# A two-layer graph network on one core: pairwise distances from a broadcast through DRAM, and seven block products for all four gate columns

## Chip, core and metric

The kernel runs on one core of a Trainium2 chip. The metric is the device time of one execution in microseconds (us). Five engines work side by side: TensorE (PE; its weight loads are listed apart as PEld), VectorE (DVE), ScalarE (ACT), GpSimd (POOL) and SyncE (SP). SP, ACT and POOL also start DMAs, and a DMA's waits stand in the queue of the engine that starts it. All data is 32-bit float.

## What is computed

There are 64 graphs of 256 nodes with 256 features. Layer 0 is a degree-normalised convolution with a residual and a layer norm. Layer 1 takes its output `x` and the mask `adj`:

```python
h = relu(bn(conv1d(xc, conv1_w)))                 # xc = x transposed, width 1
x_conv = relu(bn(conv1d(h, conv2_w)) + xc)        # width 17 along the nodes
s = x @ w_se.T + b_se                             # 3 columns
dist = |s_n - s_m|^2                              # 256 x 256 per graph
A = exp(-dist) * adj
x_nmp = A @ relu(x @ w_msg.T + b_msg)
gi = [x_conv, x_nmp] @ w_ih.T + b_ih              # 3 x 256 columns: r, z, n
gh = x @ w_hh.T + b_hh
r, z = sigmoid(gi_r + gh_r), sigmoid(gi_z + gh_z)
n = tanh(gi_n + r * gh_n)
out = layernorm(x + (1 - z) * n + z * x)
```

The gates thus need four column groups of 256: r and z (both inputs summed), n from `gi` and n from `gh`.

## The kernel before

**Stages.** The width-17 convolution is done by Fourier transforms over all graphs of a quarter (`Q` = 16 graphs) at a time, four quarters in all. For each quarter, graphs first pass `layer0` (L346) and `layer1` (L431), which leaves the transformed `h` in a large tile, and the inputs of the gates in DRAM (`xn_d`, `x1_d`). Then `products` (L557) multiplies the frequencies by weights streamed from DRAM (`load_u`, L529), in twelve steps; `real_transform`, `complex_begin` and `complex_end` (L731) transform back on VectorE alone and write `xc_d`; last, `gru` (L832) computes the gates of each graph and stores the output.

**Overlap.** These stages are Python generators that yield after each piece, and the end of the file interleaves their pieces. While one quarter is multiplied and transformed back, the first `AHEAD` graphs of the next one run, into a second tile `V2` (12 graphs ahead in the first quarter, 6 in the next two); the other graphs of that quarter follow with four "early" gates; the other twelve gates ("late") go beside the next quarter's products and transform. `paced` (L942) places pieces of the transform after marked instructions: each `mark` adds 1.2, 1.0, 0.65 or 1.35 pieces (`RATES`, L1042). What is then left of the transform is run without such cover (L1087 to L1090). The fourth quarter's sixteen gates run alone at the end.

**The order on each engine** is not just the order of the code. A planner lays out each engine's queue ahead of the run, from the order of the code and from estimated durations; in the trace VectorE runs L906 of a gate ahead of its L888, which the code has first. On the chip each queue is then worked off in order: an instruction that waits holds everything behind it.

**Distances** (L449 to L506). `scols` takes the three columns of `s` and their negative half-norms; PE transposes it (L493), ACT and VectorE copy the two halves to SBUF (L495, L497), two matmuls of 32 rows give the products (L504), ACT takes exp (L505), VectorE multiplies by the transposed `adj` in `adjT` (L506), and PE forms `x_nmp` in the same graph (L513). `xn_d` is written in one DMA from ACT's queue (L518).

**Gates** (L832 to L911). The columns r and z are one 2 x 2 block product by Strassen's method: seven block products of three matmuls of 256 columns each (L846), with four input sums on POOL (L825 to L830) and four weight differences. The two n groups are plain: twelve matmuls of 256 columns (L883). All accumulate in a PSUM pool of four banks (`accbank`), and VectorE adds the parts. `trz`, `nn`, `first` and `gn` hold the gate values; the layer norm of the output (L313) ends the chain.

The compiler splits every such matmul in two instructions in the trace, so 33 matmuls of a gate are 66 instructions.

Of the kernel before, what the change touches and what calls it, by code (L numbers as in the profile page):

```python
# [9 lines left out]
F32 = mybir.dt.float32  # L10
AF = mybir.ActivationFunctionType
ALU = mybir.AluOpType
# [14 lines left out]
def kernel(  # L27
# [93 lines left out]
    vectors = const.tile([16, P], F32, name="bn_in")  # L121
# [21 lines left out]
    scols = const.tile([P, NCH, P], F32, name="scols")  # L143
    nc.gpsimd.memset(scols, 0.0)
    for c in (NSE, 32 + NSE):
        nc.gpsimd.memset(scols[:, :, c : c + 1], 1.0)
# [4 lines left out]
    wrz = const.tile([P, 7, HALF, D], F32)  # L151
    B11, B21, B22, T1, T2, T3, T4 = range(7)
    wn = const.tile([P, 3 * DCH, D], F32)
    brz_t = const.tile([P, 2, D], F32)
    bn_t = const.tile([P, 2, D], F32)
# [53 lines left out]
    def tables(pool):  # L209

        period = pool.tile([1, 25 * FL], F32, name="period")
# [8 lines left out]
        fwd_row = pool.tile([1, FL, FL], F32, name="fwd_row")  # L220
        w_row = pool.tile([1, TAPS, 2, NU], F32, name="w_row")
# [30 lines left out]
        row = w_row.rearrange("p t h n -> p t (h n)")  # L252
        for c in range(GC):
            nc.sync.dma_start(wt[c * TR : (c + 1) * TR], row[:, :TR])
        nc.sync.dma_start(wt[GC * TR :], row[:, TR : TR + 1].to_broadcast([1, GC, 2 * NU]))
# [85 lines left out]
    XN = {}  # L341
    ALONE = set()
# [3 lines left out]
    def layer0(g):  # L346
# [3 lines left out]
        adjT = work.tile([P, NCH, 3, P], F32, name="adjT", bufs=3)  # L350
# [71 lines left out]
    def x1_transposed(g):  # L422
        x1 = X1.pop(g)
        xn = XN[g] = work.tile([P, 2 * DCH, N], F32, name="xn")
        p = bank("p_x1T").rearrange("p (k n) -> p k n", k=DCH)
        for k in range(DCH):
            for c in range(NCH):
                nc.tensor.transpose(p[:, k, c * P : (c + 1) * P], x1[:, c, k * P : (k + 1) * P], ident)
        nc.scalar.copy(xn[:, :DCH], p)  # L429

    def layer1(g, place):  # L431

        if g not in XN:
            x1_transposed(g)
        xn, adjT = XN.pop(g), ADJT.pop(g)
        x1T = xn[:, :DCH]
        yield

        h = work.tile([P, NCH, D + NSE], F32, name="h", bufs=1)
        for c in range(NCH):  # L440
# [5 lines left out]
            mark(nc.vector.tensor_tensor(h[:, c, :], p, bc1, op=ALU.add))  # L446
        nc.scalar.activation(h[:, :, :D], h[:, :, :D], AF.Relu)  # L447

        s3 = h[:, :, D:]  # L449
        cols = scols.rearrange("p c (q r) -> p c q r", r=32)  # L450
        nc.vector.tensor_copy(cols[:, :, :, :NSE], s3.unsqueeze(2).to_broadcast([P, NCH, 4, NSE]))
        sq3 = small.tile([P, NCH, NSE], F32, name="sq3")
        nc.vector.scalar_tensor_tensor(sq3, s3, -1.0, s3, op0=ALU.mult, op1=ALU.mult)
        nsq = small.tile([P, NCH], F32, name="nsq")
        nc.vector.tensor_reduce(nsq, sq3, AX.X, ALU.add)
        nc.vector.tensor_scalar(
            cols[:, :, 2:4, NSE], nsq.unsqueeze(2).to_broadcast([P, NCH, 2]), 0.5, None, op0=ALU.mult
        )
        yield
        msg = work.tile([P, NCH, D], F32, name="msg", bufs=1)  # L460
# [7 lines left out]
        nc.scalar.activation(msg, msg, AF.Relu)  # L468
        yield
# [19 lines left out]

        yield  # L490
        p = bank("p_rows")
        for c in range(NCH):
            nc.tensor.transpose(p[:, c * P : (c + 1) * P], scols[:, c, :], ident)  # L493
        dl = work.tile([64, N], F32, name="dist_l", bufs=1)
        nc.scalar.copy(dl, p[0:64, :N])  # L495
        dr = work.tile([64, N], F32, name="dist_r", bufs=1)
        nc.vector.tensor_copy(dr, p[64:P, :N])  # L497
        yield

        aT = work.tile([P, NCH, 2, P], F32, name="aT", bufs=1)  # L500
        for c in range(NCH):
            rows = slice(32 * c, 32 * c + 32)
            p = bank("p_dist")[:, :N]
            nc.tensor.matmul(p, dl[rows, c * P : (c + 1) * P], dr[rows, :], start=True, stop=True)  # L504
            nc.scalar.activation(aT[:, c].rearrange("p n q -> p (n q)"), p, AF.Exp, bias=nsq[:, c : c + 1], scale=2.0)  # L505
        mark(nc.vector.tensor_mul(aT, aT, adjT[:, :, 0:3:2, :]))  # L506
        yield
        if g in ALONE:
            x1_transposed(g + 1)
        p = bank("p_nmp").rearrange("p (k n) -> p k n", k=DCH)  # L510
        for k in range(DCH):
            for mc in range(NCH):
                nc.tensor.matmul(  # L513
                    p[:, k, :], msg[:, mc, k * P : (k + 1) * P], aT[:, mc].rearrange("p n q -> p (n q)"),
                    start=mc == 0, stop=mc == NCH - 1,
                )
        nc.scalar.copy(xn[:, DCH:], p)
        nc.scalar.dma_start(xn_d[g], xn)  # L518
# [114 lines left out]
    def turned(re, im, angle):  # L633


        t = freq.tile([P, 2, D], F32, name="turn", bufs=3)
# [7 lines left out]
    def real_transform():  # L644
# [17 lines left out]
        for i, x, y in ((1, 9, 13), (2, 10, 14), (3, 15, 11)):  # L662
            angle = math.pi * ORDER[i] / 8
            t = freq.tile([P, 2, D], F32, name="turn", bufs=3)
# [50 lines left out]
    def output(q, n, re, im):  # L715
# [4 lines left out]
        t = freq.tile([P, 2, D], F32, name="turn", bufs=3)  # L720
# [79 lines left out]
    def transposed(g):  # L800
# [3 lines left out]
        if in_blocks(g):  # L804
            behind(nc.vector.transpose(xcT.rearrange("p k (s r) -> p k s r", r=RB), CONV.pop(g)))
            nc.gpsimd.tensor_tensor(xcT, xcT, inputs[:, :DCH], op=ALU.add)
# [15 lines left out]
    def input_sums(g):  # L822
# [9 lines left out]
    def gru(g):  # L832
# [41 lines left out]
        for c in range(NCH):  # L874
            terms = [(inputs[:, k, c * P : (c + 1) * P], wn[:, k]) for k in range(3 * DCH)]
            if c == 0 and following:
                input_sums(g + 1)
# [280 lines left out]
```

## Time and profile before

| | |
|---|---|
| median of 3 runs | 2149.64 us (2147.59 to 2150.93) |
| span of the profiled execution, first to last instruction | 2152.3 us |
| PE, PEld busy | 2052.7 us, 1735.8 us |
| DVE, ACT, POOL busy | 1581.6, 841.9, 664.8 us |
| moved by DMA | 298.30 MB, 139 GB/s on average |
| granted TensorE clock | 0.990 on average |

The profile lists no separate time for the profiled execution other than its span, which lies 2.7 us (0.12%) above the median of the runs; sums below are made against the span. Busy time is the union of an engine's instructions. A matmul of 128x256 is listed with some 380 ns, but consecutive ones overlap, so what one takes of PE is the distance between starts. "Releaser" means the work whose end released a wait.

### The profile page before, as it was taken

How to read it: one execution, taken by the hardware profiler on the slowest of the kernel's cores; microseconds unless marked ns; L12 is line 12 of the kernel's file. 1: busy time of each engine (PE TensorE's matmuls, PEld its weight loads, DVE VectorE, ACT ScalarE, POOL GpSimd, SP SyncE). 2: the span in 40 equal slices, each digit the busy share in tenths (PEclk: the TensorE clock that was granted, in tenths of full speed). 3: DMA queues.
4: the chain of work that ended last, by engine and by line, in shares of the span. 5: the costliest groups of instructions: out<-in, count | busy, mean ns of one | idle time of the engine just before them, and what ended most of it. 6: DMA issues, size and time to landing. Idle time of an engine off the chain costs nothing.

```text
span 2152.3 us, 28977 instructions
## 1 busy us (share of the span) xinstructions
PE 2052.7 (95%) x9693; PEld 1735.8 (81%) x9693; DVE 1581.6 (73%) x3719; ACT 841.9 (39%) x1857; POOL 664.8 (31%) x640
## 2 busy tenths in 40 slices
PE   7999999887999999899999999999999998999997
PEld 5888788776888888788888888777888887788886
DVE  5555578775568788775656988876566889988887
ACT  4665643456431123445552122446553112222222
POOL 2444310121431244213322133323231123444442
PEclk9999999999999999999999999999999999999999
DMA  4766666434346644233326654324324744443331
GB/s 122 235 196 197 198 194 207 142 132 134 96 146 203 203 110 128 93 112 113 113 94 190 205 157 113 118 98 133 102 88 136 243 116 122 119 102 99 94 84 54
DMA packets 295085, 298.30 MB, mean 139 GB/s; under 512 B 76414, under 2 KB 273618, under 8 KB 294938
## 3 DMA queue, kind: packets, MB, share of 16 engines
q1 hardware_dynamic: 235050, 200.46, 30.9%
q10 hardware_dynamic: 44480, 67.39, 8.8%
q0 software_dynamic: 15408, 28.61, 6.1%
q8 instruction: 77, 1.26, 0.2%
q14 instruction: 70, 0.57, 0.1%
HBM read 193.28 MB, written 103.06 MB: 138 GB/s over the span
## 4 chain that ended last, share of the span: by engine, by line
PE 44%; DVE 12%; issue 9%; POOL 6%; ACT 4%; DMA 2%; ACTq 0%; SPq 0%; POOLq 0%; DVEq 0%
PE p_rz L846 14%; PE p_n L883 8%; PE p_k L539 7%; PE p_out L409 2%; PE p_nmp L513 2%; PE p_hT L399 2%; PE p_dft L480 2%; POOL ln_rs L323 2%; PE p_conv L443 1%; PE p_msg L464 1%; PE p_dist L504 1%; POOL sums L826 1%; POOL sums L825 1%; DMA u<-ud 1%; POOL xc_g L796 1%
## 5 line engine op out<-in xcount | busy, mean ns | idle before, releaser
L883 PE MATMUL p_n<-wn,inputs 128*128 128x256 f32 x1536 | 355.1, 385 | 13.4 <-DVE first L859 13.2
L846 PE MATMUL p_rz<-wrz,sums 128*128 128x256 f32 x1536 | 348.6, 380 | 1.3 <-DVE gn L888 0.8
L883 PEld LDWEIGHTS p_n<-wn,inputs 128*128 128x128 f32 x1536 | 288.5, 192 | 64.2 <-DVE first L859 20.9
L846 PEld LDWEIGHTS p_rz<-wrz,sums 128*128 128x128 f32 x1536 | 290.0, 190 | 44.5 <-issue 5.2
L846 PE MATMUL p_rz<-wrz,inputs 128*128 128x256 f32 x1152 | 271.6, 379 | 1.0 <-ACT inputs L808 1.0
L323 POOL TENSOR_TENSOR ln_rs<-ln_rs,neg_half 128x2 f32<-128x2 f32 x129 | 99.1, 768 | 510.9 <-DVE ln_rs L322 464.0
L846 PEld LDWEIGHTS p_rz<-wrz,inputs 128*128 128x128 f32 x1152 | 217.6, 190 | 31.1 <-ACT inputs L808 1.2
L895 ACT ACTIVATE nn<-gn 128x256 f32<-128x256 f32 x128 | 53.3, 417 | 332.1 <-DVE gn L892 331.7
L539 PE MATMUL p_k<-u,VM 128*128 128x256 f32 x736 | 175.2, 380 | 2.7 <-DMA u<-ud 1.9
L369 POOL TENSOR_TENSOR dis<-deg,neg_half 128x2 f32<-128x2 f32 x64 | 46.1, 720 | 423.6 <-DVE deg L367 393.1
L333 ACT ACTIVATE x_g<-x_g,ln_mr,ln_rs 128x256 f32<-128x256 f32 x128 | 70.0, 593 | 241.5 <-DVE ln_mr L331 241.5
L539 PEld LDWEIGHTS p_k<-u,VM 128*128 128x128 f32 x736 | 138.1, 190 | 24.4 <-DMA u<-ud 4.1
L480 PE MATMUL p_dft<-fwd,h 128*128 128x240 f32 x512 | 120.2, 379 | 25.9 <-ACT h L447 24.6
L399 PE MATMUL p_hT<-adjT,x 128*128 128x256 f32 x512 | 129.8, 397 | 14.0 <-DVE adjT L381 7.6
L825 POOL TENSOR_TENSOR sums<-inputs 128x384 f32<-128x384 f32 x64 | 67.1, 1048 | 239.0 <-ACT inputs L816 206.3
L480 PEld LDWEIGHTS p_dft<-fwd,h 128*128 128x128 f32 x512 | 95.2, 192 | 47.6 <-ACT h L447 41.2
L506 DVE TENSOR_TENSOR aT<-aT,adjT 128x512 f32<-128x512 f32 x64 | 44.6, 698 | 118.2 <-ACT aT L505 118.1
L443 PE MATMUL p_conv<-wc,xn 128*128 128x259 f32 x512 | 125.8, 388 | 4.3 <-ACT xn L429 4.3
L392 POOL TENSOR_TENSOR x_t<-x_t,b_t 128x512 f32<-128x512 f32 x64 | 85.4, 1334 | 142.6 <-ACT x L391 97.4
L409 PE MATMUL p_out<-w,hT 128*128 128x256 f32 x512 | 123.1, 383 | 1.4 <-ACT hT L404 0.7
L464 PE MATMUL p_msg<-wmsg,xn 128*128 128x256 f32 x512 | 121.4, 380 | 0.0
L513 PE MATMUL p_nmp<-aT,msg 128*128 128x256 f32 x512 | 121.2, 379 | 0.2 <-DVE aT L506 0.2
(157 smaller groups left out, 3910.2 us busy)
## 6 DMA issues: line engine op xcount, KB each, us to landing
u<-ud SPq DMA_DIRECT2D x284, 256.0 KB
xn_d<-xn ACTq DMA_DIRECT2D x64, 512.0 KB
inputs<-xn_d SPq DMA_DIRECT2D x64, 512.0 KB
ud<-u_set POOLq DMA_DIRECT2D x39, 480.0 KB, 6.1
adj_t<-in_adj_dram SPq DMA_DIRECT2D x64, 256.0 KB
x_t<-in_x_dram SPq DMA_DIRECT2D x64, 256.0 KB
x_d<-x ACTq DMA_DIRECT2D x64, 256.0 KB
xc_d<-VM SPq DMA_DIRECT2D x64, 256.0 KB
```

The source lines that it names most:

```text
L323: nc.gpsimd.tensor_tensor(rs[:, : len(chunks)], rs[:, : len(chunks)], neg_half[:, : len(chunks)], op=ALU.pow)
L392: nc.gpsimd.tensor_tensor(x_t, x_t, b0_t.unsqueeze(1).to_broadcast([P, NCH, D]), op=ALU.add)
L399: nc.tensor.matmul(p[:, k, :], x1[:, mc, k * P : (k + 1) * P], adjT[:, mc, 1 - mc : 3 - mc, :].rearrange("p n q -> p (n q)"), start=mc == ...
L409: nc.tensor.matmul(p[:, c, :], hT[:, k, c * P : (c + 1) * P], w0[:, k, :], start=k == 0, stop=k == DCH - 1)
L443: nc.tensor.matmul(p, x1T[:, k, c * P : (c + 1) * P], wc1[:, k, :], start=k == 0, stop=k == DCH - 1)
L464: nc.tensor.matmul(p[:, c, :], x1T[:, k, c * P : (c + 1) * P], wmsg[:, k, :], start=k == 0, stop=k == DCH - 1)
L480: nc.tensor.matmul(p[:, t0 * FL : t1 * FL], h[:, c, k * P : (k + 1) * P], fwd[:, first : first + t1 - t0, :].rearrange("p t f -> p (t f)") ...
L513: nc.tensor.matmul(p[:, k, :], msg[:, mc, k * P : (k + 1) * P], aT[:, mc].rearrange("p n q -> p (n q)"), start=mc == 0, stop=mc == NCH - 1,)
L539: nc.tensor.matmul(p[:, j * D : (j + 1) * D], v[:, k, :], u[:, k, :], start=k == 0, stop=k == DCH - 1)
L825: nc.gpsimd.tensor_tensor(S[:, 0], A21, A22, op=ALU.add)
L846: nc.tensor.matmul(p[:, j * D : (j + 1) * D], a[:, k], wrz[:, b, k], start=k == 0, stop=k == HALF - 1)
L883: nc.tensor.matmul(p[:, o * D : (o + 1) * D], lhsT, w, start=j == 0, stop=j == len(part) - 1)
```

## The change

- **Distances without matmuls.** A new generator `adjacency` writes the three columns (`own`, 128 x 2 x 3) to DRAM (`s_d`), and a second DMA on SP's queue reads them back into every partition (`s_all`, 128 x 256 x 3, 384 KB). ACT then computes, for each of the three columns and two chunks, `Square(own - s_all)`; POOL adds the three squares; one exp of 512 columns on ACT, and the multiplication by `adjT` on VectorE as before. `scols`, the transposes, the copies and the matmuls L493 to L505 go.
- **`x_nmp` is deferred.** `messages()` forms it in the next graph's `layer1`, after that graph's `msg` matmuls. `xn_d` is written in two DMAs from ACT's queue, x1's part when it is transposed, `x_nmp` later. The transposition of graph g+1 is always made in graph g (before: for the 12 graphs of the first `AHEAD` only).
- **All four gate columns by seven block products.** Each column half holds 4 groups of 128 (hidden n, r, z, input n). A product is three matmuls of 384 columns: the first, on x1's features, covers hidden n, r, z; the others cover r, z, input n. Two products accumulate onto banks that VectorE has read before (`p5`, `p7`). The gate values lie in one tile `G`, with one buffer; one of the additions is POOL's. `tanh` is taken over r and z of the whole graph at once, and the n part in one sequence of 512 columns.
- **Memory and order.** 4 graphs ahead, not 6, in the second and third quarter; `layer1` has four pieces instead of seven, and `PLACES` follows; `adjT` gets 4 buffers, `turn` 2, `sums` four tiles of one buffer; tables are built in the memory of the gate weights.

```diff
+    def adjacency(g, own, adjT, msg):
+        everyone = work.tile([P, N, NSE], F32, name="s_all", bufs=1)
+        nc.sync.dma_start(s_d[g].rearrange("(c p) s -> p c s", p=P), own)
+        flat = s_d[g].rearrange("n s -> (n s)")
+        nc.sync.dma_start(everyone, bass.AP(tensor=flat.tensor, offset=flat.offset, ap=[[0, P], [NSE, N], [1, NSE]]))
+        yield
+        aT = work.tile([P, NCH, N], F32, name="aT", bufs=1)
+        for d in range(NSE):
+            to = aT if d == 0 else work.tile([P, NCH, N], F32, name="square", bufs=1)
+            for c in range(NCH):
+                nc.scalar.activation(
+                    to[:, c], everyone[:, :, d], AF.Square, bias=own[:, c, d : d + 1], scale=-1.0
+                )
+            if d:
+                nc.gpsimd.tensor_tensor(aT, aT, to, op=ALU.add)
+        nc.scalar.activation(aT, aT, AF.Exp, scale=-1.0)
+        blocks_of = aT.rearrange("p c (n q) -> p c n q", q=P)
+        mark(nc.vector.tensor_mul(blocks_of, blocks_of, adjT[:, :, 0:3:2, :]))
+        NMP.append((g, aT, msg))
+    def messages():
...
+        g, aT, msg = NMP.pop(0)
...
+        nc.scalar.copy(nmp, p)
+        nc.scalar.dma_start(xn_d[g][:, 1 : 1 + DCH], nmp)
...
+        own = small.tile([P, NCH, NSE], F32, name="own")
+        nc.vector.tensor_copy(own, h[:, :, D:])
         nc.scalar.activation(h[:, :, :D], h[:, :, :D], AF.Relu)
...
+        weighing = adjacency(g, own, adjT, msg)
+        next(weighing)
+        yield
...
+        messages()
+        x1_transposed(g + 1)
         yield
...
+        run(weighing)
         yield
...
+        def product(a, b, p=None):
+            first = p is None
+            if first:
+                p = accbank("p_g")
             for k in range(HALF):
                 nc.tensor.matmul(
+                    p[:, : 3 * HD] if k == 0 else p[:, HD:], a[:, k], wall[:, b, k].rearrange("p t d -> p (t d)"),
+                    start=first and k == 0, stop=True, skip_group_check=not first or k > 0,
+                )
+            return p
...
+        p1 = product(A11, B11)
+        p2 = product(A12, B21)
+        p6 = product(S[1], T2)
         yield
...
+        mark(nc.vector.tensor_add(quarter(0, 0), p1, bias(0)), 1)
+        nc.vector.tensor_add(quarter(1, 0), quarter(0, 0), p6)
+        nc.gpsimd.tensor_tensor(quarter(0, 1), quarter(1, 0), bias(1), op=ALU.add)
+        nc.vector.tensor_add(quarter(0, 0), quarter(0, 0), p2)
+        p5 = product(S[0], T1)
+        p7 = product(S[2], T3)
+        mark(nc.vector.tensor_add(quarter(1, 1), quarter(0, 1), p5), 1)
...
+        product(S[3], B22, p5)
+        mark(nc.vector.tensor_add(quarter(1, 1), quarter(1, 1), p7), 1)
...
+        product(A22, T4, p7)
+        nc.vector.tensor_add(quarter(0, 1), quarter(0, 1), p5)
+        mark(nc.vector.tensor_add(quarter(1, 0), quarter(1, 0), p7), 1)
...
-    PLACES = (("other",), ("layer0",), (), (), ("layer0",), ("other", "layer0"), ())
+    PLACES = (("layer0",), ("other",), ("layer0",), ("other", "layer0"))
...
-                scope, AHEAD, V2 = open_ahead(6)
+                scope, AHEAD, V2 = open_ahead(4)
```

## Prediction

> **What bounds the kernel now.** I read the engine totals and the chain first, then the busy time by stage, then the timeline where the change acts.
>
> ```profile
> PE 2052.7 (95%) x9693; PEld 1735.8 (81%) x9693; DVE 1581.6 (73%) x3719; ACT 841.9 (39%) x1857; POOL 664.8 (31%) x640
> PE 44%; DVE 12%; issue 9%; POOL 6%; ACT 4%; DMA 2%; ACTq 0%; SPq 0%; POOLq 0%; DVEq 0%
> L883 PE MATMUL p_n<-wn,inputs 128*128 128x256 f32 x1536 | 355.1, 385 | 13.4 <-DVE first L859 13.2
> ```
>
> PE is busy all but 99.6 us, and heads the chain. The busy time by stage (columns: PE, PEld, DVE, ACT, POOL, clock, DMA share):
>
> ```profile
> 0.00:260.00 260.00, 241.04 (x1146) 197.45 (x1147) 142.29 (x469) 148.22 (x346) 107.84 (x112) 0.98 0.62 194
> 260.00:610.00 350.00, 322.78 (x1539) 268.22 (x1538) 242.69 (x646) 167.62 (x376) 79.50 (x76) 0.99 0.48 148
> 610.00:1145.00 535.00, 519.87 (x2476) 441.40 (x2475) 390.46 (x915) 210.06 (x467) 155.93 (x150) 0.99 0.44 130
> 1145.00:1650.00 505.00, 491.51 (x2349) 418.27 (x2348) 374.74 (x871) 194.84 (x431) 144.70 (x139) 1.00 0.43 131
> 1650.00:1870.00 220.00, 207.67 (x953) 177.41 (x952) 198.67 (x390) 43.23 (x88) 62.15 (x54) 0.99 0.54 161
> 1870.00:2152.30 282.30, 269.79 (x1239) 233.08 (x1237) 232.72 (x430) 77.94 (x153) 114.68 (x109) 0.99 0.32 87
> ```
>
> Stage 1 is the first quarter's layers, 2 to 4 mix layers, products, transform and gates, 5 is products and late gates beside the last transform (DVE at 90%), 6 gates alone. PE sets the pace in all but 5; ACT is fullest in stage 1. One graph of stage 1, on PE:
>
> ```profile
> 136.85 1.89 PE L480 MATMUL p_dft<-fwd,h 128*128 128x240 f32 x8
> 138.57 0.38 PE L493 MATMUL p_rows<-ident,scols 128*128 128x128 f32 x2
> 138.79 1.89 PE L399 MATMUL p_hT<-adjT,x 128*128 128x256 f32 x8
> 140.61 0.70 PE L504 MATMUL p_dist<-dist_r,dist_l 32*128 32x256 f32 x4
> 141.24 1.99 PE L302 MATMUL p_u<-taps,dft_w 85*120 85x256 f32 x8
> ```
>
> From start to start, the transposes take 0.22 us and the distances 0.63. The same sequence returns after 16.04 us. One gate of stage 6:
>
> ```profile
> 2040.11 2.75 PE L846 MATMUL p_rz<-wrz,inputs 128*128 128x256 f32 x12
> 2042.70 5.34 PE L846 MATMUL p_rz<-wrz,sums 128*128 128x256 f32 x24
> 2045.26 1.27 POOL L806 TENSOR_TENSOR inputs<-inputs 128x512 f32<-128x512 f32 x1 [4.41 <-DMA inputs<-xn_d]
> 2045.37 1.70 DVE L907 SCALAR_TENSOR_TENSOR nn<-trz,nn 128x512 f32<-128x512 f32 x1 [0.48 <-ACT nn L895]
> 2054.58 1.67 PE L846 MATMUL p_rz<-wrz,inputs 128*128 128x256 f32 x7
> ```
>
> A gate takes 2054.58 - 2040.11 = 14.47 us; twelve instructions take 2.59, so one takes 0.2158 us, 66 take 14.24, and 0.23 is waiting.
>
> **What the Trainium skill says.** (1) "TensorE: Matmul & The Clock Gate", Back-to-back issue gap: a warm matmul of N columns takes N/2.4 + 2.5 ns. With two passes per listed instruction, N = 512 gives 215.8 ns: the trace agrees. (2) "Advanced Engine Details and Errata", VectorE Performance Modes and GPSIMD Details: POOL shares an SBUF interface with VectorE and conflicts with its instructions on two SBUF inputs. The trace agrees: L907 above has to wait for POOL's L806 to end, and takes 1.70 us instead of 0.69. (3) "DMA: Bandwidth & Descriptors", Two DMAs through the same engine are not ordered: a DMA that reads what another wrote must wait for its semaphore on the issuing engine. So the broadcast holds SP's queue; no line of before shows this wait. (4) "ScalarE: Activation LUTs", Table sets: cheap functions are in every set; square is listed beside relu and identity in the precision table. Before loads a table once (1.283 us); no line shows Square.
>
> **The change, part by part.**
>
> *Distances off PE.* 0.22 + 0.63 = 0.85 us for each of 64 graphs: **-54 us** of PE, all in stages 1 to 4.
>
> *Gates.* 42 instructions of 384 columns: by (1), 768/2.4 + 2.5 = 322.5 ns, 13.55 us instead of 14.24; 0.69 x 64 = -44 if all is taken. About half the gates (32) stand in PE-bound stretches: -22. Some 14 stand beside a transform, where VectorE is at 90 to 95%: it keeps seven PSUM additions of 0.68 and five SBUF operations of 0.69 = 8.2 us, against 4.8 + 4 x 0.42 + 3 x 0.69 = 8.5 before: nothing. In stage 6 (18 gates) a new loop counts, because `G` has one buffer: two additions 1.44, POOL's addition 1.27 and a hop 0.1, addition 0.75, two products of 1.94 and an end of 0.17 each, addition 0.75, tanh of 1024 some 1.2, two operations 1.4, tanh 0.73, two operations 1.4 = 13.3 us until `G` is free, 14.5 if the layer norm's statistics (1.2) go first. That is no shorter than PE's 13.55; I take 14.3: 0.2 x 18 = -3. Together **-25 us** (both ends: -44, and +50 below).
>
> *Order.* `p_dft` now follows `msg`, `x_nmp` and a transposition. PE lost 24.6 us at `p_dft` to ACT's relu (L447): I take half back, **-12** (0 to -24).
>
> *ACT.* Removed per graph: L495 0.37, two exps 0.84. Added: six Squares with a per-partition bias, a pair by L391's pair 0.91 (the stride of 12 bytes is not shown; 0.91 to twice that): 2.73; exp of 512 as L447, 0.63; a second issue 0.34. Net +2.5 us. In stage 1 ACT's row of work, issues included, sums to 11.3 us of 16.04; it becomes 13.8 of 15.2. ACT works in order and PE needs its copies, and the squares wait for the broadcast and twice for POOL. I take 1.0 us of PE per graph, 14 graphs: **+14** (0 to +31, the 2.2 us at which ACT alone would set the pace with its waits). In stages 2 to 4 ACT has over 4 us free per graph: 0.3 x 50 = **+15** (0 to +100).
>
> *The broadcast and SP.* The bias broadcast of the same shape (L1009, 384 KB) is issued at 239.47 and read at 243.36: 3.9 us. With the copy `own` 0.2, an issue 0.4 and a small write, for which I take 3 (1 to 4; the last store of the program lies 3.7 before its end), squares can begin 7.5 us after the convolution; adding POOL's and ACT's 6 us, exp and product end after some 14. `x_nmp` is needed a graph later, after 17 to 20 us. So it is hidden, barely in stage 1, where DMA is at 62% on average. Behind the broadcast on SP stand the loads of graphs, gates and `u`: graphs are loaded three ahead, and SP already waits 301 us for L110's buffers; `u` is six buffers of 0.86 us ahead, and only some five graphs run beside products that have no gates. Nothing, or 10 us if that cover is gone. The extra issues of gate weights (16 instead of 11, 0.4 each) lie in SP's idle time.
>
> *Fewer graphs ahead.* A graph carries six marks before and after. First quarter: products take 36 pieces of the layers; a graph has 7 + 3 pieces before and 4 + 3 after, so 5.1 graphs go there instead of 3.6, and 6.9 instead of 8.4 are left: 50 pieces of the transform placed instead of 60. Second and third: 7.5 late gates x 5 x 0.65 + 4 x 6 = 48 of 62 pieces, before 64 of 64. A piece is two operations, 0.85 us; some 10 per quarter lose their cover, 8 us each; a late gate hides half: **+12** (0 to +25).
>
> *POOL and the shared port.* POOL gets two additions of 1.27 per graph and one per gate, VectorE loses 0.29 + 0.17 + 0.16 + 0.17 + 0.43 and gains a copy of 0.2, so 1.0 less per graph. Where VectorE is tight the waits outweigh this: **+10** (-10 to +40).
>
> `turn` with two buffers is touched by VectorE alone; splitting `xn_d` delays nothing that is read soon. Zero.
>
> Sum: -54 - 25 - 12 + 14 + 15 + 12 + 10 = **-40 us**: a span of 2112.3. The median of before lies 2.7 below its span: **2110 us**, own range 2070 to 2143.
>
> **Rivals.** *A: ACT is held by the broadcast* (slower). The squares stand in ACT's queue where the planner expects the data; if it lands later, hT, x1T and the transform copies behind it wait, and PE with them. Without the two ACT terms the sum is -69, so from 1.1 us of PE per graph on it is a loss; at 1.7 us, 64 x 1.7 - 69 = +40: 2190. For it: DMA full in stretches of stage 1, two DMAs in series, POOL twice in the chain. Against: 4 us free on ACT elsewhere, a graph of slack. *B: the gate loop sets the pace.* Waits for POOL's port in the four final SBUF operations make the loop 16 us; 18 gates lose 27 instead of gaining 3, the 14 beside a transform 21: 2161. Against: POOL's sums are done before the tail. *C: all of it comes through*, gates and waits in full: -54 - 44 - 24 + 12 = -110: 2040. *D: Square needs its own table*: two loads of at least 1.28 us per graph make ACT the bound: about 2270. The page speaks against it.
>
> **Chances.** Forecast 0.42 (0.01 of it no change), A 0.27, B 0.18 (faster 0.02, same 0.04, slower 0.12), C 0.09, D 0.04. About 0.2% (4 us) is what measurement can tell from no change. Faster 0.41 + 0.02 + 0.09 = 0.52, same 0.05, slower 0.12 + 0.27 + 0.04 = 0.43. The range, 2040 to 2200, leaves out half of C, the upper third of A, and D.
>
> **What would show it.** L846's successor with 42 x 0.322 us per gate; stage 1's period (15.2 to 16.2: right; over 16.5: A); ACT's waits for `s_all` (A if above 2 us per graph); the period of the last gates (14.3, or B at 16); a single table load; idle PE around the ends of the transforms. I am wrong if PE's idle time grows by more than its work shrinks: from 100 to over 200 us.

## The result, and the profile after

The changed kernel takes **2464.99 us** (median of 4 runs, 2453.21 to 2468.39) against 2148.61 us (2146.57 to 2150.93): a ratio of **1.1465, 95% interval 1.1435 to 1.1494**. It is 316 us slower; forecast were 2110 us and a range that ends at 2200. The profiled execution has a span of 2463.2 us against 2152.3, at a mean granted TensorE clock of 0.936 against 0.990.

The engine totals, the chain and three groups on the page of the kernel after:

```profile
PE 2077.0 (84%) x7773; PEld 1484.4 (60%) x7773; DVE 1509.9 (61%) x3337; ACT 998.5 (41%) x1985; POOL 880.1 (36%) x829
PE 34%; DVE 21%; POOL 15%; issue 14%; DMA 8%; ACT 7%; SPq 0%; POOLq 0%; ACTq 0%; DVEq 0%
L855 PE MATMUL p_g<-wall,sums 128*128 128x384 f32 x1536 | 557.0, 506 | 112.0 <-DVE G L879 61.1
L455 POOL TENSOR_TENSOR aT<-aT,square 128x512 f32<-128x512 f32 x128 | 163.1, 1274 | 446.4 <-ACT square L451 284.5
L451 ACT ACTIVATE square<-s_all,own 128x256 f32<-128x256 f32 x256 | 150.9, 637 | 104.5 <-DMA s_all<-s_d 54.7
```

TensorE has 1920 instructions fewer and yet more busy time, and its idle time rose from 99.6 to 386.2 us. I read both from one cause, waiting. Busy time multiplied by the mean clock is nearly the same in every kernel with these 7773 instructions (2077.0 x 0.936 = 1944; in two of the experiments below, e7 2012.2 x 0.963 = 1938, e13 1982.4 x 0.974 = 1931). So the work did shrink: 2052.7 x 0.990 = 2032 before, 1944 after. At the clock of before the 1944 would take 1964 us. The span's growth of 311 us is then 287 us of new waiting and 113 us of lower clock, less 89 us of work saved. The Trainium skill ("TensorE: Matmul & The Clock Gate", The HAM clock gate) says that the clock is gated by how busy TensorE has lately been; the trace agrees in kind, as the stretches show (columns as in the prediction; cut at the first and last product of each quarter's transform):

```profile
0.00:360.70 360.70, 278.97 (x1161) 224.80 (x1162) 144.25 (x444) 209.65 (x444) 153.06 (x145) 0.91 0.57 164
493.40:779.40 286.00, 218.44 (x815) 163.02 (x815) 156.88 (x391) 150.73 (x306) 100.42 (x94) 0.86 0.43 115
779.40:889.80 110.40, 108.38 (x433) 80.44 (x432) 89.69 (x168) 18.68 (x33) 24.90 (x24) 1.00 0.69 211
889.80:1346.20 456.40, 391.53 (x1471) 280.50 (x1470) 271.16 (x629) 219.96 (x444) 175.72 (x166) 0.93 0.42 114
1986.30:2463.20 476.90, 387.39 (x1157) 216.71 (x1155) 345.92 (x632) 97.98 (x162) 188.52 (x182) 0.97 0.30 83
```

Where TensorE waits, the clock is 0.86 to 0.97; in the second products (the third line), where it hardly waits, it is 1.00. The share of idle time alone doesn't set it: the last stretch is idle for 19% at 0.97, the one above it for 14% at 0.93. That the waiting causes the lower clock is the page's account; it fits these stretches, but no run separates the two. The same cuts, in us:

| kernel | to products 1 | products 1 | to 2 | 2 | to 3 | 3 | to 4 | 4 | to the end |
|---|---|---|---|---|---|---|---|---|---|
| before | 285.2 | 100.0 | 250.7 | 110.9 | 404.1 | 109.1 | 394.9 | 83.0 | 414.4 |
| after | 360.7 | 132.7 | 286.0 | 110.4 | 456.4 | 109.5 | 444.1 | 86.5 | 476.9 |

Every stretch with layers grew, 75.5 us in stage 1 alone, and so did the last one, which has gates and no layers (62.5). Of the products the first grew, since five graphs now pass beside it instead of three; the others moved by 3.5 us at most.

One graph of stage 1 in the timeline of the kernel after:

```profile
136.77 0.18 DVE L490 COPY own<-h 128x6 f32<-128x6 f32 x1
136.98 0.38 SPq L443 DMA_DIRECT2D s_d<-own  x1
141.28 0.35 SPq L445 DMA_DIRECT2D s_all<-s_d  x1
146.87 1.17 ACT L451 ACTIVATE aT<-s_all,own 128x256 f32<-128x256 f32 x2 [1.11 <-DMA s_all<-s_d]
149.19 1.26 POOL L455 TENSOR_TENSOR aT<-aT,square 128x512 f32<-128x512 f32 x1 [4.92 <-ACT square L451]
150.42 3.33 POOL L313 TENSOR_TENSOR u_set<-u_set,u_set 120x1024 f32<-120x1024 f32 x1
153.72 1.25 POOL L455 TENSOR_TENSOR aT<-aT,square 128x512 f32<-128x512 f32 x1
155.00 0.63 ACT L456 ACTIVATE aT<-aT 128x512 f32<-128x512 f32 x1 [2.54 <-POOL aT L455]
155.66 0.69 DVE L458 TENSOR_TENSOR aT<-aT,adjT 128x512 f32<-128x512 f32 x1 [3.00 <-ACT aT L456]
156.50 1.75 PE L468 MATMUL p_nmp<-aT,msg 128*128 128x256 f32 x7 [2.13 <-DVE aT L458]
156.68 0.41 DVE L488 TENSOR_TENSOR h<-p_conv,bc 128x259 f32<-128x259 f32 x1
157.73 0.19 DVE L490 COPY own<-h 128x6 f32<-128x6 f32 x1
```

From `own` to the next `own` it is 20.96 us, where a graph took 16.04. The path is a ring: the write and the broadcast land 10.1 us after `own`; the squares, an addition on POOL, `u_set`'s 3.33 us that stand in POOL's queue, the second addition, Exp and the mask take 9.5; and behind the mask, on VectorE's queue, stands the addition that makes the next graph's `h` (L488) and so its `own`. The idle times in brackets show each engine waiting in turn: ACT 2.54, DVE 3.00, PE 2.13. For ten graphs in a row (from 95.1 us on) the period is 20.8 to 24.7 us, and each `own` begins 1.2 to 2.5 us after the mask's end. In the later stretches the work of gates stands in between; there I have not followed the ring link by link. `u_set` runs in stage 1 alone:

```profile
L313 POOL TENSOR_TENSOR u_set<-u_set,u_set x13: 3320/3326/3412, 42.6 to 307.8; 120x1024 f32<-120x1024 f32 x13
```

(thirteen times; shortest, median and longest in ns; first and last start in us.)

### The profile page after: what moved, and what is told of

It is laid out like the page before. It is cut to its first block, busy times and chain, and to the rows that moved or that the text cites. A ratio compares the mean times of both kernels' runs of the same rounds, so it can differ in the third digit from the quotient of the medians.

```text
span 2463.2 us, 25628 instructions
## 1 busy us (share of the span) xinstructions
PE 2077.0 (84%) x7773; PEld 1484.4 (60%) x7773; DVE 1509.9 (61%) x3337; ACT 998.5 (41%) x1985; POOL 880.1 (36%) x829
## 4 chain that ended last, share of the span: by engine, by line
PE 34%; DVE 21%; POOL 15%; issue 14%; DMA 8%; ACT 7%; SPq 0%; POOLq 0%; ACTq 0%; DVEq 0%
PE p_g L855 17%; PE p_k L548 6%; POOL aT L455 5%; PE p_nmp L468 3%; POOL sums L837 3%; PE p_msg L499 2%; POOL ln_rs L328 2%; DMA s_all<-s_d 2%; ACT square L451 2%; PE p_hT L404 2%; DMA u<-ud 2%; DMA s_d<-own 2%; PE p_dft L518 1%; POOL x_t L397 1%; POOL G L875 1%
## 5 line engine op out<-in xcount | busy, mean ns | idle before, releaser
L855 PE MATMUL p_g<-wall,sums 128*128 128x384 f32 x1536 | 557.0, 506 | 112.0 <-DVE G L879 61.1
L855 PEld LDWEIGHTS p_g<-wall,sums 128*128 128x128 f32 x1536 | 294.9, 196 | 332.9 <-POOL sums L837 77.1
L855 PE MATMUL p_g<-wall,inputs 128*128 128x384 f32 x1152 | 406.8, 498 | 11.1 <-DVE G L884 10.0
L455 POOL TENSOR_TENSOR aT<-aT,square 128x512 f32<-128x512 f32 x128 | 163.1, 1274 | 446.4 <-ACT square L451 284.5
L855 PEld LDWEIGHTS p_g<-wall,inputs 128*128 128x128 f32 x1152 | 224.2, 196 | 159.2 <-DVE G L884 14.9
L328 POOL TENSOR_TENSOR ln_rs<-ln_rs,neg_half 128x2 f32<-128x2 f32 x129 | 97.7, 758 | 355.4 <-DVE ln_rs L327 273.7
L837 POOL TENSOR_TENSOR sums<-inputs 128x384 f32<-128x384 f32 x128 | 138.5, 1084 | 216.7 <-PE p_g L855 154.4
L499 PE MATMUL p_msg<-wmsg,x1T 128*128 128x256 f32 x512 | 152.3, 448 | 71.7 <-DVE x L419 67.1
L451 ACT ACTIVATE square<-s_all,own 128x256 f32<-128x256 f32 x256 | 150.9, 637 | 104.5 <-DMA s_all<-s_d 54.7
L468 PEld LDWEIGHTS p_nmp<-aT,msg 128*128 128x128 f32 x512 | 111.7, 225 | 118.6 <-DVE aT L458 52.7
L499 PEld LDWEIGHTS p_msg<-wmsg,x1T 128*128 128x128 f32 x512 | 108.5, 222 | 100.6 <-DVE x L419 76.0
L336 DVE SCALAR_TENSOR_TENSOR ln_mr<-ln_mv,ln_rs 128x2 f32<-128x2 f32 x129 | 71.8, 556 | 120.4 <-POOL ln_rs L328 120.2
L485 PE MATMUL p_conv<-wc,x1T 128*128 128x259 f32 x512 | 127.9, 392 | 16.1 <-ACT V L523 7.9
L458 DVE TENSOR_TENSOR aT<-aT,adjT 128x512 f32<-128x512 f32 x64 | 50.8, 793 | 134.9 <-ACT aT L456 123.6
```

The source lines that it names most:

```text
L328: nc.gpsimd.tensor_tensor(rs[:, : len(chunks)], rs[:, : len(chunks)], neg_half[:, : len(chunks)], op=ALU.pow)
L451: nc.scalar.activation(to[:, c], everyone[:, :, d], AF.Square, bias=own[:, c, d : d + 1], scale=-1.0)
L455: nc.gpsimd.tensor_tensor(aT, aT, to, op=ALU.add)
L468: nc.tensor.matmul(p[:, k, :], msg[:, mc, k * P : (k + 1) * P], aT[:, mc], start=mc == 0, stop=mc == NCH - 1,)
L485: nc.tensor.matmul(p, x1T[:, k, c * P : (c + 1) * P], wc1[:, k, :], start=k == 0, stop=k == DCH - 1)
L499: nc.tensor.matmul(p[:, c, :], x1T[:, k, c * P : (c + 1) * P], wmsg[:, k, :], start=k == 0, stop=k == DCH - 1)
```

## Experiments: which part, and how much

My theory was that two losses add: the distances' ring (some 245 us, the growth of the stretches ahead of the last), and in the last stretch a loop over `G` (some 63). The rivals were that one of them is nearly all of it, or that the new order and the fewer graphs ahead cost the time.

| run | us | ratio to before, 95% interval |
|---|---|---|
| e1 distances on TensorE | 2261.8 | 1.0522, 1.0506 to 1.0538 |
| e2 old gates | 2384.4 | 1.1087, 1.1071 to 1.1104 |
| e3 before, four ahead | 2156.6 | 1.0047, 1.0033 to 1.0061 |
| e4 one trip | 2332.6 | 1.0844, 1.0823 to 1.0866 |
| e5 products reordered | 2247.6 | 1.0456, 1.0436 to 1.0476 |
| e6 order only | 2174.5 | 1.0120, 1.0103 to 1.0137 |
| e7 additions on VectorE | 2353.0 | 1.0953, 1.0936 to 1.0970 |
| e8 trips nobody reads | 2329.3 | 1.0832, 1.0809 to 1.0854 |
| e9 gates' tails later | 2204.4 | 1.0262, 1.0248 to 1.0276 |
| e10 order, spread | 2154.4 | 1.0039, 1.0027 to 1.0052 |
| e11 one trip, additions on VectorE | 2227.9 | 1.0373, 1.0359 to 1.0387 |
| e12 order, six ahead | 2149.1 | 1.0002, 0.9993 to 1.0011 |
| e13 squares a graph later | 2246.8 | 1.0476, 1.0459 to 1.0494 |
| e14 e13 and e9 | 2193.2 | 1.0215, 1.0195 to 1.0234 |
| e15 e13, old gates | 2168.9 | 1.0093, 1.0073 to 1.0112 |
| e16 e15, two pieces a step | 2174.6 | 1.0125, 1.0105 to 1.0146 |

**e1, distances back on TensorE**; inside `adjacency`:

```diff
-        everyone = work.tile([P, N, NSE], F32, name="s_all", bufs=1)
...
-        nc.scalar.activation(aT, aT, AF.Exp, scale=-1.0)
+        for c in range(NCH):
+            nc.tensor.transpose(p[:, c * P : (c + 1) * P], scols[:, c, :], ident)
...
+            nc.tensor.matmul(p, dl[rows, c * P : (c + 1) * P], dr[rows, :], start=True, stop=True)
+            nc.scalar.activation(aT[:, c], p, AF.Exp, bias=nsq[:, c : c + 1], scale=2.0)
```

> The kernel after with the distances back on TensorE: the row of transposes, two copies and two small products inside adjacency, ScalarE's Exp straight from their bank. The deferred message product, the early x1 transpose, the four graphs ahead and the new gates are kept. Distance theory (the chain of broadcast, squares and POOL's additions fills the layer phases): the growth of the stretches before the last gates, 75.5 + 32.7 + 35.3 + 52.5 + 49 = 245 us, goes but for what the new gates cost beside the transforms (30 to 60), so 2220 to 2280. Gate theory (most of the growth is the new gates' pace): not under 2350. Order theory (deferral and fewer graphs ahead cost the time): not under 2400.

**e2**, the gates' functions, weights and `xn` layout of before in the kernel after.

```diff
-        G = gate.tile([P, NCH, 2, 4, HD], F32, name="G", bufs=1)
+        trz = gate.tile([P, 4, D], F32, name="trz", bufs=1)
+        nn = gate.tile([P, NCH, D], F32, name="nn", bufs=1)
...
```

> The kernel after with the gates of before (six blocks by Strassen, the n columns by plain products); the new distances, the order and the four graphs ahead are kept. Distance theory: only the last gates' 62.6 us and a little beside the transforms come back, 2370 to 2405. Gate theory: 2150 to 2250. Order theory: 2390 to 2460.

**e3**, in the kernel before:

```diff
-                scope, AHEAD, V2 = open_ahead(6)
+                scope, AHEAD, V2 = open_ahead(4)
```

> The kernel before with four graphs opened ahead in place of six, and nothing else. Distance theory: 2149 to 2170, since the loads still run well ahead. Order theory (the shorter queue of open graphs lets TensorE run dry between the transforms): over 2220.

Measured 2261.8, 2384.4 and 2156.6: each in the interval of the distance theory. Undoing the distances brings 203 us, undoing the gates 81, and four graphs ahead cost 8. In e1 the last stretch is still 474.2 us, in e2 it is 412.6: that growth belongs to the gates (the page of e2 is 64 us below that of after there, and some 21 in all other stretches).

**e6 and e10, the order alone.** e6 joins e1 and e2, so that only the order and the four graphs ahead are left of the change. In e10 the transposes and copies stand ahead of `p_dft` and the distance products behind it; in e1 and e6 I had put them back to back.

```diff
         nc.vector.tensor_copy(dr, p[64:P, :N])
+        yield
...
         x1_transposed(g + 1)
+        next(weighing)
         yield
```

> The kernel after with both the distances of before on TensorE and the gates of before: what is left of the change is the order (messages a graph later, the next x1's transposes early, xn sent in two parts) and four graphs ahead. By the prediction's terms -12 for the order and the measured +8 for four graphs: 2135 to 2150. If the order itself costs (a graph's work spread over two, more of it left when a transform begins): 2165 to 2190. If the parts simply add, 2149 + (2262 - 2149) + (2384 - 2149) - (2465 - 2149) gives 2181 for what the two others don't explain, so about 2180.

> The order alone (2174.5 us) with the row of transposes and its two copies ahead of the transform's products and the small distance products behind them, where they stood back to back and TensorE waited 43 us for dist_r. If the order itself is neutral and this placing of mine cost: 2140 to 2160. If the order costs (two graphs more pass beside the first quarter's products, which grow by 21 us, and the stretch behind them, which finds two graphs fewer, gets only 2 us shorter): 2165 to 2175.

e6 gave 2174.5, in the interval for an order that itself costs; e10 gave 2154.4, in the one for a neutral order. So 20 us of e6 were my placing: TensorE waited 43.4 us for `dist_r`, in e10 2.3. In e1, which has the same placing, it waited 32.5 us; what that cost e1 was not run. Against e3, which also has four ahead, the order is worth -2 us, not measurable. With e10 as the base, the change is made up so: 8 for four ahead, -2 for the order, **230 for the distances** (e2 less e10), **81 for the gates** (after less e2). These are steps of one path from before to after, so that their sum has to be the whole. What tests that the parts add is the other path: the gates cost 87 beside TensorE's distances (e1 less e6), and the distances, with my placing, 203 beside the new gates (after less e1) and 210 beside the old (e2 less e6).

**e12 and e16, two pieces a step** beside the first products: e12 on e10, with six graphs ahead too; e16 on e15, which is told below.

```diff
-                run(take(begin, 3))
+                run(take(begin, 2))
...
-                scope, AHEAD, V2 = open_ahead(4)
+                scope, AHEAD, V2 = open_ahead(6)
```

> As the order alone with its distance products spread, with six graphs ahead again and two pieces a step beside the first quarter's products in place of three, since a graph has fewer pieces in this order. If the 21 us by which that stretch grew were work moved out of the stretch behind, that had been hidden there beside the transform's end: 2125 to 2150, under the kernel before. If the order costs elsewhere: 2155 to 2170.

> The same with two pieces a step beside the first quarter's products in place of three. If these two give what they gave with the six graphs ahead on TensorE's distances (5 us together): within 5 us of the run before it. If the products' stretch only hands its work on: the same time as that run, within 3 us.

e12 gave 2149.1, no different from before, and e16 was 5.8 us slower than e15, outside both readings. My reason for the edit falls, though e12 lies in its interval: in e12 the first products shrank from 116.3 to 97.7 us, but the stretch behind grew from 241.9 to 271.1. What e12 gained came in the later stretches (403.5 to 392.5, 396.0 to 389.0), where six are ahead.

## Experiments: what the distances wait for

**e4, one trip**: the columns are written and spread for the first graph only. The kernel leaves out the distances of the other graphs, which take that graph's columns; what the engines do is otherwise the same.

```diff
-        everyone = work.tile([P, N, NSE], F32, name="s_all", bufs=1)
+        if not ONCE:
+            ONCE.append(work.tile([P, N, NSE], F32, name="s_all", bufs=1))
...
+        everyone = ONCE[0]
```

> The kernel after with the s columns spread to all partitions once, for the first graph; the 63 other trips through DRAM are left out (so the distances of the other graphs are taken against the first graph's columns). Squares, additions, Exp and all else are kept. If the distance chain costs by the trip through DRAM (SP waiting for the first DMA with the loads behind it, ScalarE waiting for the second): 2250 to 2300. If it costs by ScalarE's squares and POOL's additions in queues that other work stands in: 2400 to 2450. Gate theory: as the kernel after, 2450 to 2465.

**e8**: in e4, the trips again, into a tile that nobody reads, and with 112 of the 256 nodes, since there is no room for more.

```diff
+        else:
+            landed = work.tile([P, 112, NSE], F32, name="landed", bufs=1)
+            nc.sync.dma_start(s_d[g].rearrange("(c p) s -> p c s", p=P), own)
...
+            nc.sync.dma_start(landed, bass.AP(tensor=flat.tensor, offset=flat.offset, ap=[[0, P], [NSE, 112], [1, NSE]]))
```

> The kernel of the one trip (2332.6 us; all graphs' squares are taken against the first graph's columns, so the other graphs' distances are left out), with the write of own and the broadcast put back on SP's queue for every graph (112 of the 256 nodes, for want of room), into a tile that nobody reads. If the trip cost 132 us because SP stands in it with the other loads behind: 2420 to 2460. If it cost because ScalarE waits for the columns to land: 2330 to 2345.

e4 gave 2332.6, under "2400 to 2450" and above "2250 to 2300": neither reading alone. The trip is worth 132 us, not all. e8 gave 2329.3: SP waits for the writes as in after (161.1 us in 61 waits, 163.1 in after), and nothing is lost. So what costs is that ScalarE, and all behind it, waits for the landing. That a broadcast of the full size takes nothing from other transfers e8 doesn't show, as it moves less than half the bytes; e13 below, with full trips and a later reader, speaks for it.

**e7, additions on VectorE**, and **e11**, the same edit in e4 (so it too leaves out the other graphs' distances).

```diff
-                nc.gpsimd.tensor_tensor(aT, aT, to, op=ALU.add)
+                nc.vector.tensor_tensor(aT, aT, to, op=ALU.add)
```

> The kernel after with the two additions of a graph's squares on VectorE in place of GpSimd, nothing else. If GpSimd's queue (1.27 us an addition, with u_set's 3.3 us standing between the two) makes up the part of the distances' cost that the trip through DRAM does not, about 70 us: 2395 to 2420. If ScalarE's squares are that part: 2450 to 2470. If VectorE, with two more instructions a graph ahead of x, is then the later one: over 2470.

> The kernel after with both cuts: the additions of the squares on VectorE, and one trip through DRAM for the first graph alone (the other graphs' distances are left out). Apart they brought 112 and 132 us of the 203 us that the distances cost. If the two lie on one chain, whose slack is used up once and whose rest is ScalarE's squares: 2280 to 2310. If the squares cost nothing by themselves: 2250 to 2270, the level of the distances on TensorE. If the chain is not left after either cut: the effects add and it falls below 2240.

e7 gave 2353.0, 112 us less and below all I had expected: having the additions on GpSimd costs nearly as much as the trip. e11 gave 2227.9, the third case: the two cuts nearly add (237 us against 132 + 112). In the waits of the kernel after, and then of e7:

```profile
DVE aT L458 <- ACT aT L456: 123.6, 42, 11.4
ACT aT L456 <- POOL aT L455: 95.9, 61, 3.3
PE p_nmp L468 <- DVE aT L458: 77.2, 26, 6.3
```

```profile
ACT aT L451 <- DMA s_all<-s_d: 80.6, 39, 6.0
ACT aT L456 <- DVE aT L455: 49.4, 46, 3.8
PE p_nmp L468 <- DVE aT L458: 45.1, 21, 6.1
DVE aT L455 <- ACT square L451: 211.6, 75, 9.4
```

(us in all, times, longest.) Without POOL in the chain, Exp and the product `p_nmp` wait little more than half as long. VectorE's 123.6 us at the mask fall to 3.8, but that wait is not gone: it stands at the additions now, for the squares.

My theory had put the cost of the additions down to `u_set` between them. That is not so: e7 brought 23.6 us in stage 1, the only stretch with `u_set`, but 17.7, 33.8 and 28.2 in the stretches to products 2, 3 and 4. What is shorter everywhere is the addition itself (first after, then e7):

```profile
L455 POOL TENSOR_TENSOR aT<-aT,square x128: 1252/1267/1720, 46.9 to 1902.7; 128x512 f32<-128x512 f32 x128
L455 DVE TENSOR_TENSOR aT<-aT,square x128: 673/693/3844, 46.5 to 1795.6; 128x512 f32<-128x512 f32 x128
```

Two of them at 0.69 us in place of 1.27 are 1.16 us a graph, 74 of the 112 us if all of it stands in the path; this is an estimate from the medians. How much of the rest is POOL's queue, no run separates.

**e13, squares a graph later**, with every trip and the right columns, and the additions on VectorE.

```diff
+        messages()
         msg = work.tile([P, NCH, D], F32, name="msg")
...
         x1_transposed(g + 1)
+        if WEIGH:
+            run(WEIGH.pop(0))
+        WEIGH.append(adjacency(g, own, adjT, msg))
+        next(WEIGH[0])
...
-        run(weighing)
```

> The kernel after, all graphs' distances from their own columns again and one trip through DRAM for each, with the additions on VectorE, and a graph's squares, Exp and mask put behind the next graph's message product (the trip has a whole graph's time to land), its neighbours' messages another half graph later. If the trip costs by its latency alone: the level of the one-trip run with the additions on VectorE, 2220 to 2245. If the 63 transfers or SP's waits cost by themselves, or the later messages give new waits: 2290 to 2350.

> The kernel with the additions on VectorE and the squares behind the next graph (2246.8 us), with the gates of before: distances without TensorE, all waits for the trip cured, four graphs ahead. Against the order alone with its products on TensorE (2154.4 us): if the 54 us of TensorE's work taken away come through, 2095 to 2120. If ScalarE's squares and VectorE's additions, in queues that also feed TensorE, give them back: 2145 to 2170. By addition of the parts measured (2246.8 less the 80.6 us of the gates) 2166.

e13 gave 2246.8, 106 us below e7, 2 us above the interval of "latency alone" and far from the other. Leaving the trips out brings 125 us here (e7 less e11), so most of the trip can be hidden by moving its reader. e15, the same with the gates of before, gave 2168.9, in the second interval: what e2 has at 2384.4 is cured by 216 us, and still the 54 us do not come through, for e10 with its distances on TensorE has 2154.4. The engine totals of e10, then of e15:

```profile
PE 2050.7 (95%) x9693; PEld 1750.9 (81%) x9693; DVE 1544.0 (72%) x3783; ACT 842.1 (39%) x1855; POOL 670.6 (31%) x640
```

```profile
PE 2004.2 (92%) x9309; PEld 1726.1 (80%) x9309; DVE 1597.0 (74%) x3591; ACT 1005.5 (46%) x2111; POOL 668.0 (31%) x637
```

TensorE's busy time is 46.5 us less; its idle time is 164.7 us instead of 104.0, 60.7 more. The spans differ by that, 14.2 us. ACT has 163 us more work in a queue that also carries the copies `hT` and `x1T`; in e15 TensorE waits 16.4 us for `hT` and 16.3 for `x`, 32.6 for `adjT`, 29.9 for the mask. In e10 it waits 10.5 for `x`, 2.3 for `adjT`, and 22.8 for `scols`, which e15 no longer has. So I take ACT's and VectorE's queues for the reason; no run shows which of the two.

## Experiments: what the gates wait for

One gate of the last stretch after, in the timeline:

```profile
2297.33 0.69 DVE L890 TENSOR_TENSOR G<-G,p_g 128x512 f32<-128x512 f32 x1 [1.25 <-PE p_g L855]
2298.05 1.06 ACT L897 ACTIVATE G<-G 128x1024 f32<-128x1024 f32 x1 [4.48 <-DVE G L890]
2301.74 1.09 DVE L907 SCALAR_TENSOR_TENSOR G<-G 128x512 f32<-128x512 f32 x1 [0.70 <-ACT G L903]
2303.59 0.75 DVE L325 BATCH_NORM_STATS2 ln_st<-x_g 128x6 f32<-128x256 f32 x2
2304.34 0.66 DVE L873 TENSOR_TENSOR G<-p_g,ball 128x512 f32<-128x512 f32 x1
2306.59 1.26 POOL L875 TENSOR_TENSOR G<-G,ball 128x512 f32<-128x512 f32 x1
2307.81 0.71 POOL L328 TENSOR_TENSOR ln_rs<-ln_rs,neg_half 128x2 f32<-128x2 f32 x1
2308.48 1.00 POOL L837 TENSOR_TENSOR sums<-inputs 128x384 f32<-128x384 f32 x1
2308.55 0.95 DVE L336 SCALAR_TENSOR_TENSOR ln_mr<-ln_mv,ln_rs 128x2 f32<-128x2 f32 x1 [1.30 <-POOL ln_rs L328]
2309.43 0.68 DVE L879 TENSOR_TENSOR G<-G,p_g 128x512 f32<-128x512 f32 x1
2310.25 2.17 PE L855 MATMUL p_g<-wall,sums 128*128 128x384 f32 x6 [2.29 <-DVE G L879]
```

The same product of the gate before starts at 2293.19: the period is 17.06 us. TensorE's 42 instructions take 0.322 each, from start to start (a group of 16 lasts 5.32 us, its last instruction 0.49, so 4.83 / 15), together 13.5 us; 3.5 us is waiting. The loop goes from the last addition (L890) through the tail and the layer norm's statistics on VectorE to the next gate's first addition (L873), over POOL's addition of the bias (L875), to L879, on which the next product waits.

**e5, the products in another order**, so that L879 (now L892) has more time; on e1.

```diff
         p1 = product(A11, B11)
-        p2 = product(A12, B21)
         p6 = product(S[1], T2)
+        p5 = product(S[0], T1)
...
         p7 = product(S[2], T3)
+        p2 = product(A12, B21)
```

> The kernel with the distances back on TensorE (2261.8 us), and in it only the order of a gate's seven products changed: P1, P6, P5, P7, P2, then S3*B22 and A22*T4, in place of P1, P2, P6, P5, P7 and these two; the same products, additions and buffers. If the last gates are slow because TensorE waits in that chain of additions (3.5 us in each 17.06 us period), the period falls to 13.6 to 14.5 us, the last quarter from 474 to about 425 us and the whole to 2190 to 2215. If VectorE, ScalarE and GpSimd together set the pace (the additions, the transpose and the layer norm need their 17 us anyway), nothing moves: 2255 to 2265.

**e9, the last gates' tails behind the next gate's first additions**, on e5, with a second `G`.

```diff
+        if TAIL:
+            next(TAIL[0])
...
+        if TAIL:
+            run(TAIL.pop(0))
```

> The kernel with the distances on TensorE and the gates' products reordered (2247.6 us), and in the last sixteen gates only the tail of a gate (from the first product with r to the layer norm) put behind the next gate's first additions, with a second G and a second place for the result in the transform's buffer, which is idle by then. If the pace of the last gates, still some 16 us after the reordering, is one chain that closes over G (a gate's last addition, its tail on VectorE and ScalarE, the layer norm, and only then the next gate's first addition, two more and the product that waits for them): the period falls to 13.5 to 14.5 and the whole to 2200 to 2225. If an engine's occupancy or the loads set the pace: 2240 to 2250.

e5 gave 2247.6, only 14 us, between its two intervals: TensorE's order is the smaller part. I took the loop to close over `G` on VectorE's queue whatever TensorE does first; e9 tests it. It gave 2204.4, another 43 us, in the interval for such a loop. With the loop open, the period is TensorE's own work (timeline of e9, where the first addition is L914):

```profile
2108.02 5.97 PE L896 MATMUL p_g<-wall,sums 128*128 128x384 f32 x18
2108.70 0.68 DVE L914 TENSOR_TENSOR VM<-p_g,ball 128x512 f32<-128x512 f32 x1
2113.82 2.10 PE L896 MATMUL p_g<-wall,inputs 128*128 128x384 f32 x6
2122.25 0.69 DVE L914 TENSOR_TENSOR VM<-p_g,ball 128x512 f32<-128x512 f32 x1
```

2122.25 - 2108.70 = 13.55 us.

**e14, both cures.**

> The same with the gates' products reordered and, in the last sixteen gates, the tails behind the next gate's first additions. If the two losses are separate, the 57 us that this brought with the distances on TensorE come off here too: 2165 to 2190. If the distances' chain and the gates' share a bound beside the transforms: 2200 or more.

e14 gave 2193.2, between its two readings, 3 us above the first: the tails and the order bring 54 us here and 57 on e1, so the two losses are separate. Of 316 us 272 are cured; no version that I ran is faster than the kernel before. Why the cured gates and distances together don't gain the work that they save stays open.

## Why the prediction was wrong

- **Distances off PE, -54**: right as work (46.5 us less between e10 and e15), wrong as time, since the idle time that came with it was larger in every version that I ran.
- **The broadcast and SP, "So it is hidden, barely in stage 1"**: this step failed. Squares were to begin 7.5 us after the convolution and began 10.1 after `own`; Exp and the product with the mask were to end after some 14 and ended after 19.6. The write took 4.3 us from issue to the broadcast's issue, not 3, and the broadcast 5.6, not 3.9. The rest of the error is in the 6 us for "POOL's and ACT's": with the mask they took 9.5. The pairs of squares take 1.17 us, not 0.91, the mask 0.69, and in stage 1 `u_set` holds back the second addition by 2.1 us (the squares that it needs end at 151.66, it begins at 153.72). Worse, the slack was measured against a graph's period as if that stood still. The next trip starts behind this graph's mask on VectorE, so a late mask delays the trip that it should have been compared with. Measured: 132 us for the landing (e4), 112 for having the additions on POOL (e7), where the terms for ACT (+14, +15) and POOL (+10) sum to 39. SP's part, "nothing, or 10 us", was right as far as e8 goes.
- **Gates, -25**: 0.322 us an instruction was right. The loop was seen but mis-sized: at most 14.5, taken 14.3; it is 17.06. Left out were what stands between its links in the queues: L906 between two steps of the tail (0.6), POOL's sums ahead of L875 (0.8), and the layer norm's POOL step and L336, which keep L879 1.6 us after L875's end (2307.85 to 2309.43). Waits for POOL's port are a part of it: L907 takes 1.09 instead of 0.69, and L336, on two values a row, 0.95 beside POOL's L837, where it takes 0.16 with POOL at rest. The gates cost 81 us; in the stretches beside layers the hoped-for 22 did not come either.
- **Order, -12**: -2 (e10 against e3). **Fewer graphs ahead, +12**: +8 (e3). **Square's duration**: 1.17 us a pair, within its bounds. **Its table**: one load of 1.283 us in the whole program, so D was excluded rightly.
- **The rivals**: A was true in kind; B's slow loop came, with the port wait that it named as a part of the cause, 0.4 us, and another, 0.8 us, at an instruction that it had not named. I had set them up as alternatives with a chance each, so that the range held one or the other, not both. Their prices added, 2110 + 80 + 51, would still have fallen 224 us short. A's price was a guess of 1.7 us a graph; the distances cost 230/64 = 3.6. And my sign for A was badly chosen: ACT's waits for `s_all` are 54.9 + 54.7 us, 1.7 a graph, under the 2 that I had named, because most of the delay shows as waits of POOL, VectorE and TensorE for each other. The period above 16.5 and the idle time above 200 us told rightly.
- **Not in the sum at all**: the clock. An idle TensorE was counted once, as idle; here 287 us of new waiting came with 113 us of slower products.

## What to carry over

A chain that hops DMA, ScalarE, GpSimd, VectorE costs little in busy time and much in queues: follow it to the instruction that starts the *next* round, and take that ring, with all that stands in each queue between its links, as the period. Before taking matmuls away to spare TensorE, ask what its shorter work is then waiting for: here, in stage 1, 0.85 us a graph of TensorE was replaced by a ring of 21 us. And check a cause that one graph's timeline suggests against all stretches: `u_set` looked like the reason and stood in one of the five stretches with layers. Where two rivals are independent they add; give the range room for both.

## What the hardware showed unexpectedly

- A write of 3 KB to DRAM and its broadcast to 128 partitions took 4.3 and 5.6 us from issue to use in the graph shown, 10 us in all (medians of the 64 graphs 4.1 and 5.5), where a broadcast of the same size had taken 3.9 before. The Trainium skill ("SBUF — State Buffer", The DMA setup-cost knee) puts the fixed part of any transfer at some 2 us; the 3 KB write took twice that here, and the measurement decides.
- The same matmul list took 1982 us at a mean clock of 0.974 and 2077 at 0.936; the mean of a `p_nmp` product rose from 379 to 447 ns.
- Two additions a graph on GpSimd, the emptier engine (36% busy against 61%), cost 112 us of the span more than on VectorE. There they took 0.69 us in the median instead of 1.27; twenty of the 128 took 0.9 to 3.8, each while an instruction of GpSimd ran, five of them 2.5 to 2.8 beside `u_set`.
- A VectorE instruction on two values a row (L336) took 0.16 us with GpSimd at rest and 0.95 beside GpSimd's L837 of 1.00 us, in seventeen gates running, inside the loop that sets the pace.
